# The early table of a routed feed-forward layer, made after eleven of sixteen groups instead of twelve

## The chip, the cores and the metric

The kernel runs on one core of a Trainium2 chip. The metric is the device time of one execution in microseconds (us). Before the change three runs gave 2174.46, 2169.46 and 2175.39 us, a median of 2174.46 us.

## What is computed

The input is eight sequences of 1024 tokens with 256 features, all in float32. The reference does two steps, each with a layer norm in front, a layer norm behind and the input added back:

```
x = x + _layernorm(attn(_layernorm(x), Wq, Wk, Wv, Wo))
x = x + _layernorm(ffn(_layernorm(x), router_weight, router_bias, gate_up_proj, ..., down_bias))
```

The attention is causal, with 16 heads of 16 features. The feed-forward layer has eight experts of 512 hidden features. A router gives each token a softmax over the experts. The two best experts are applied to the token, and their outputs are added with the router's weights.

## The kernel before, in words

**Attention (lines 542 to 1391).** A unit is one sequence b and four heads, so there are 32 units, u = 0 to 31. One pass of the loop at line 1299 computes the row maxima of unit u (scores `sa`, line 834; reductions on VectorE, lines 844 to 888) and, beside them, the weighted values of unit u-1 (scores `sb`, line 929; exponentials on ScalarE, line 941; masks on GpSimd, line 950; products `av`, line 970). A unit has nine steps k = 0 to 8, each in two pairs of heads. The last pass, u = 32, has only the values of unit 31.

The values of a unit need its negated maxima as extra rows of the queries. `rows` (line 796) reduces and transposes them on VectorE, and four copies (line 807) bring them into the query tile. The copies go through SyncE's queue (SP below), which takes its transfers in order.

**Work between the scores.** Whatever belongs to a finished half sequence (a group of 512 tokens, 16 groups t = 0 to 15) is written as generators that give up control with `piece(...)`: the output projection and first norm (`finish`, line 1017), the router (`route`, line 1074) and the tables (`table`, line 301). They stand in a list `back` as jobs. A planner, `pump` (line 1253), runs a step of a job when each engine has credit for the step's stated cost. The order of the list decides between jobs. The instructions of TensorE (PE), VectorE (DVE) and ScalarE (ACT) stand in the order in which this planner emits them. On GpSimd (POOL), the order of the source is kept by declared dependences.

`route` ranks the experts of each token (lines 1130 to 1149), counts with two matmuls (`cps`, line 1153), forms row numbers (lines 1160 to 1183) and scatters the normalized rows of the group into a DRAM array `xsd`, sorted by expert, with eight indirect DMAs on POOL (line 1194). It does so one group after the other.

**Tables.** The experts' work is cut into tiles of 256 rows of one expert. A table says for each tile which expert and which rows of `xsd` it has. There are two. The early one is made inside `route` of a chosen group, after so many groups as `NT - LATE` says (NT = 16 groups). It has the first EARLY = 16 tiles, which are whole already. The last table is made after all 16 groups and has the rest. In both, `table` runs some 10 to 30 small VectorE instructions between three matmuls: `segps` (line 363), `firstps` (line 371) and `tabps` (line 417). The early one has a fourth, `takenps` (line 438), and only behind it is the table marked as known (line 440).

As soon as the early table is known, in the last maxima pass (u = 31), `load_early` (line 1277) reads table entries on SP and loads the rows of the first four tiles. If it isn't known at the end of that pass, the planner is left aside (lines 1383 to 1386):

```
if u == B * NG - 1 and not early:
    while NT - LATE not in known:
        emit(back, back[0])
    load_early()
```

**Experts (lines 1638 to 1738).** The tiles run one after the other: transposes `xtps` (line 1448), four quarters of gate and up products `gu` (line 1470) with VectorE, ScalarE and POOL work behind them (lines 1479 to 1492), then the down products `dn` (line 1510), a bias add on VectorE (line 1518) and two scatters of results on POOL (line 1524). `dn` of tile i-1 stands between the quarters of tile i. `load_tile` (line 1417) is called two tiles ahead and issues on SP the rows, the weights `wg` and `wd` and the biases. While i + 2 < 16, `pump` is still called between the quarters, so that the rest of the routing is done beside the first tiles. When tile 16's loads come up, at the begin of tile 14, everything left must be done (line 1669):

```
if nth + AHEAD == EARLY:
    finish_all()
```

`finish_all` (line 1270) emits all that is left of the jobs without a look at credits. Ahead of the last table `fill_tails` (line 275) writes zeros behind the rows of each expert with eight DMAs of 258 KB on SP, and tiles loaded later wait for these.

Of the kernel before, what the change touches and what calls it, by code (L numbers as in the profile page):

```python
# [58 lines left out]
def attn_moe_kernel(  # L59
# [199 lines left out]
    def ahead_of(load, group):  # L259

        tc.add_to_no_dep_group(group, load.ins)

    def loaded(ap, most, engine=mybir.EngineType.SP):
        return nc.values_load(
            ap, engines=[engine], min_val=0, max_val=most,
            skip_runtime_bounds_check_because="tables made on the chip from counts of tokens",
        )

    def slot_rows(at, n=TN):
        return xs_dram[ds(at, n * P), :].rearrange("(n p) d -> p n d", p=P)  # L270
# [4 lines left out]
    def fill_tails():  # L275
# [9 lines left out]

    LATE = 4
    tables = {
        n: const.tile([1, 2, NTILES], I32, name=f"table{n}") for n in (NT - LATE, NT)  # L290
    }

    regions = {
        n: const.tile([P, NTILES], F32, name=f"regions{n}") for n in (NT - LATE, NT)
    }
# [246 lines left out]
    with ExitStack() as attn:  # L542
# [675 lines left out]
        def emit(kind, job):  # L1218
            job.run(now)
            if job.done:  # L1220
                kind.remove(job)
# [55 lines left out]
        def load_early():  # L1277

            flat = x_buffer("early")
            for i in range(IN_X):  # L1280
                early[i] = flat[:, ts(i, XS)].rearrange("p (n d) -> p n d", n=TN)
                at = loaded(tables[NT - LATE][:, 1, i : i + 1], E * R)
                ahead_of(nc.sync.dma_start(out=early[i], in_=slot_rows(at)), "xs")
# [3 lines left out]
        with tc.manual_schedule(  # L1287
# [11 lines left out]
            for u in range(B * NG + 1):  # L1299
# [12 lines left out]
                for k in range(K):  # L1312
                    if second:

                        for c in {t[0] for t in STEPS[k][2]}:
                            while not rows_of[u - 1, c].done:
                                emit(urgent, rows_of[u - 1, c])
                    if u == B * NG - 1 and not early and NT - LATE in known:
                        load_early()
# [63 lines left out]
# [3 lines that stand above are left out]
# [22 lines left out]
    def first_weights(i):  # L1408
        tab = tables[NT - LATE if i < EARLY else NT]
        e = loaded(tab[:, 0, i : i + 1], E - 1)  # L1410
        wg = m3.tile([P, KT, 2 * FF], F32, tag="wg", name=f"wg_{i}")
        nc.sync.dma_start(
            out=wg, in_=gate_up[ds(e, 1), :, :].rearrange("o (t p) f -> p (o t) f", p=P)
        )
        begun[i] = e, wg
# [360 lines left out]
```

## Time and profile before

| | |
|---|---|
| runs, us | 2174.46, 2169.46, 2175.39 |
| the profiled execution, us | 2167.24 |
| its span in the profile, us | 2165.1 |
| PE busy | 2057.3 us, 95% of the span |
| DVE busy | 1708.3 us, 79% |
| ACT busy | 1062.7 us, 49% |
| POOL busy | 1051.7 us, 49% |
| mean granted PE clock | 0.985 |
| end of the last `sb` scores beside maxima (unit 30) | about 1347.3 us |
| the early table written (line 421) | 1352.1 us |
| first expert tile's transposes (line 1448) | 1382.3 us |
| the last table written (line 421) | 1553.9 us |

The timeline lists instructions of one engine in order of time. A row has the start, the time from the first start to the last end, the engine, the line, the operation, the tiles it writes and reads, how many records are merged in it, and in brackets how long the engine had been idle before and what ended this. A float32 matmul shows as two records. The granted clock is 1.00 at full speed. A window row has, for a stretch of time, the busy time of each engine, the mean granted clock and the DMA share.

### The profile page before, as it was taken

How to read it: one execution, taken by the hardware profiler on the slowest of the kernel's cores; microseconds unless marked ns; L12 is line 12 of the kernel's file. 1: busy time of each engine (PE TensorE's matmuls, PEld its weight loads, DVE VectorE, ACT ScalarE, POOL GpSimd, SP SyncE). 2: the span in 40 equal slices, each digit the busy share in tenths (PEclk: the TensorE clock that was granted, in tenths of full speed). 3: DMA queues.
4: the chain of work that ended last, by engine and by line, in shares of the span. 5: the costliest groups of instructions: out<-in, count | busy, mean ns of one | idle time of the engine just before them, and what ended most of it. 6: DMA issues, size and time to landing. Idle time of an engine off the chain costs nothing.

```text
span 2165.1 us, 44591 instructions
## 1 busy us (share of the span) xinstructions
PE 2057.3 (95%) x16205; PEld 1262.3 (58%) x16205; DVE 1708.3 (79%) x4091; ACT 1062.7 (49%) x2072; POOL 1051.7 (49%) x1213
## 2 busy tenths in 40 slices
PE   7999999999999999999999998999999999999995
PEld 3444444444544434434534443678888888888884
DVE  4786886986887887887888788678778888877776
ACT  3566665666666655656655665433123232222222
POOL 3421653472474455354544645456544444444443
PEclk9999999999999999999999999999999999999998
DMA  4101102112112111112111111656867777876784
GB/s 123 23 16 44 35 26 63 32 46 46 42 32 69 24 41 46 48 36 58 46 39 41 44 39 36 207 189 208 259 242 266 269 246 262 291 241 231 268 286 150
DMA packets 147096, 254.85 MB, mean 118 GB/s; under 512 B 21504, under 2 KB 106008, under 8 KB 144952
## 3 DMA queue, kind: packets, MB, share of 16 engines
q1 hardware_dynamic: 133128, 217.01, 32.5%
q0 software_dynamic: 12528, 34.36, 4.3%
q8 instruction: 129, 2.11, 0.4%
q14 instruction: 95, 0.78, 0.1%
q10 hardware_dynamic: 1216, 0.58, 0.1%
HBM read 171.13 MB, written 55.63 MB: 105 GB/s over the span
## 4 chain that ended last, share of the span: by engine, by line
PE 71%; DVE 17%; POOL 5%; issue 3%; DMA 2%; ACT 2%; SPq 0%; DVEq 0%; ACTq 0%; POOLq 0%
PE sa L834 18%; PE gu L1470 15%; PE av L970 10%; PE dn L1510 8%; PE sb L929 6%; PE pjk L740 3%; PE yps L1031 3%; PE pjq L740 3%; PE vps L726 3%; DVE mx L850 2%; DVE sa L844 2%; DVE gate L1479 1%; PE xtps L1448 1%; DVE mx L888 1%; DVE acc L1586 1%
## 5 line engine op out<-in xcount | busy, mean ns | idle before, releaser
L941 ACT ACTIVATE pT<-sb 128x512 f32<-128x512 f32 x1134 | 616.2, 595 | 394.2 <-PE sb L929 360.6
L929 PE MATMUL sb<-qP,kP 32*128 32x512 f32 (+3 forms) x3072 | 703.6, 528 | 13.8 <-ACT pT L941 11.0
L834 PE MATMUL sa<-kP,qP 32*128 32x512 f32 (+3 forms) x3072 | 655.2, 526 | 25.5 <-DVE mx L844 12.6
L1470 PE MATMUL gu<-xsT,wg 128*128 128x256 f32 (+1 forms) x2208 | 487.5, 373 | 3.3 <-ACT xsT L1450 1.9
L1470 PEld LDWEIGHTS gu<-xsT,wg 128*128 128x128 f32 x2208 | 407.6, 191 | 59.3 <-ACT xsT L1450 4.3
L850 DVE TENSOR_REDUCE mx<-sa 128x2 f32<-128x1024 f32 x256 | 310.6, 1215 | 116.7 <-PE sb L929 96.6
L950 POOL TENSOR_SCALAR_AFFINE_SELECT pT<-pT 128x512 f32<-128x512 f32 x256 | 164.6, 659 | 468.2 <-ACT pT L941 456.1
L834 PEld LDWEIGHTS sa<-kP,qP 32*128 32x128 f32 x3072 | 226.8, 185 | 248.1 <-issue 100.0
L1481 ACT ACTIVATE sig<-gate 128x256 f32<-128x256 f32 (+1 forms) x276 | 112.8, 409 | 522.2 <-DVE gate L1479 492.0
L970 PE MATMUL av<-pT,vpad 128*32 128x256 f32 (+1 forms) x5120 | 350.0, 370 | 5.0 <-DVE avs L981 3.0
L1486 POOL TENSOR_TENSOR sig<-sig,gate 128x256 f32<-128x256 f32 (+1 forms) x276 | 195.4, 715 | 321.4 <-ACT sig L1481 317.4
L929 PEld LDWEIGHTS sb<-qP,kP 32*128 32x128 f32 x3072 | 294.9, 186 | 46.2 <-ACT pT L941 20.5
L970 PEld LDWEIGHTS av<-pT,vpad 128*32 128x32 f32 x5120 | 117.1, 109 | 292.7 <-issue 233.9
L1510 PE MATMUL dn<-wd,act 128*128 128x256 f32 x1064 | 257.7, 382 | 14.0 <-DVE act L1491 11.5
L1510 PEld LDWEIGHTS dn<-wd,act 128*128 128x128 f32 x1064 | 194.6, 190 | 45.6 <-DVE act L1491 19.4
L844 DVE CUSTOM_DVE_ANT_0 sa<-sa,cmask 128x512 f32<-128x512 f32 x256 | 177.7, 699 | 40.2 <-PE sb L929 20.8
L1479 DVE TENSOR_SCALAR gate<-gu,bs 128x256 f32<-128x256 f32 (+1 forms) x276 | 128.8, 467 | 86.2 <-PE gu L1470 70.7
L1491 DVE SCALAR_TENSOR_TENSOR act<-up,sig 128x256 f32<-128x256 f32 (+1 forms) x276 | 131.9, 478 | 49.3 <-POOL sig L1486 45.5
L1194 POOL DMA_INDIRECT xsd<-xn,slots x128 | 129.1, 1009 | 64.2 <-DVE xn L1190 34.8
L1524 POOL DMA_INDIRECT ytd<-ys,places x133 | 134.9, 1014 | 48.8 <-issue 26.9
L869 ACT COPY edge<-sa 128x512 f32<-128x512 f32 x192 | 113.0, 589 | 41.1 <-DVE mx L859 19.9
L888 DVE TENSOR_REDUCE mx<-edge 128x8 f32<-128x1024 f32 x96 | 115.7, 1205 | 17.9 <-POOL edge L883 17.9
(243 smaller groups left out, 2327.4 us busy)
## 6 DMA issues: line engine op xcount, KB each, us to landing
wg<-_L_ffn_gate_up_proj_dram SPq DMA_DIRECT2D x69, 1024.0 KB
wd<-in_L_ffn_down_proj_dram SPq DMA_DIRECT2D x69, 512.0 KB
xs<-xsd SPq DMA_DIRECT2D x60, 258.0 KB
yy<-ytd SPq DMA_DIRECT2D x15, 1024.0 KB
bs<-biasd SPq DMA_DIRECT2D x69, 132.0 KB
x<-in_L_attn_x_dram SPq DMA_DIRECT2D x16, 512.0 KB
aT<-avn SPq DMA_DIRECT2D x256, 32.0 KB
x1d<-y SPq DMA_DIRECT2D x16, 512.0 KB
```

The source lines that it names most:

```text
L834: nc.tensor.matmul(ps[:, hh, ds(at, w)], lhsT=qP[r, ts(i, P)], rhs=kP[r, ds(c * QC, w)], start=True, stop=True,)
L844: nc.vector.tensor_tensor_reduce(out=ps[:, hh, :], in0=ps[:, hh, :], in1=cmask, scale=1.0, scalar=NEG, op0=ALU.add, op1=ALU.max, accum_out ...
L850: nc.vector.tensor_reduce(mx[:, heads, i, 2:3], ps, AX.X, ALU.max)
L888: nc.vector.tensor_reduce(mx[:, :, of_two(k)[0], 1], d, AX.X, ALU.max)
L929: nc.tensor.matmul(banks[hh][:, ds(at, QC - off)], lhsT=kP[r, ts(j, P)], rhs=qP[r, ds(c * QC + off, QC - off)], start=True, stop=True,)
L941: nc.scalar.activation(pT[:, 2 * pair + hh, :], banks[hh], AF.Exp)
L950: in_order(nc.gpsimd.affine_select(out=d, in_=d, compare_op=ALU.is_ge, fill=0.0, base=0, pattern=[[0, HG], [1, P]], channel_multiplier=-1,))
L970: nc.tensor.matmul(av[ds(hh * HS, HS), ds(off + a - at, z - a)], lhsT=vp[:, j, ds((g * HG + hh) * VS, HS)], rhs=pT[:, hh, a:z],  start=c n ...
L1470: nc.tensor.matmul(ps[:, half, :w], lhsT=wg[:, kt, ds(half * FF + f * P, P)], rhs=xT[:, kt, :], start=(kt == 0), stop=(kt == KT - 1),)
L1479: nc.vector.tensor_scalar(gt, ps[:, 0, :w], bs[:, f : f + 1], LIMIT, ALU.add, ALU.min)
L1486: in_order(nc.gpsimd.tensor_tensor(sg, sg, gt, ALU.mult))
L1510: nc.tensor.matmul(pss[n][:, 0, :], lhsT=act[:, f, ts(n, P)], rhs=wd[:, f, :], start=(f == 0), stop=(f == FT - 1),)
```

## The change

```
@@ -285,7 +285,7 @@
-    LATE = 4
+    LATE = 5
     tables = {
         n: const.tile([1, 2, NTILES], I32, name=f"table{n}") for n in (NT - LATE, NT)
     }
```

`LATE` has no other use than to name the early table, so this table is made behind the routing of the eleventh group (t = 10) instead of the twelfth (t = 11). The number of tiles that it hands out stays 16. The counts of the twelfth group no longer enter it. The last table still counts all groups. The same instructions are issued, apart from one constant block that `memset` clears (40 columns instead of 32 at line 356), but the jobs stand in another order, and so the planner places what follows elsewhere.

More of the change, by code (lines that the diff above doesn't have):

```diff
@@ L283, in fill_tails @@
             apart(nc.sync.dma_start(out=slot_rows(at), in_=zeros), "xs")
-    LATE = 4
+    LATE = 5
     tables = {
```

## The prediction

> **What bounds the kernel now.** I read the page first, then the timeline of PE and DVE around the two tables, then windows of the same stretches.
>
> ```profile
> PE 2057.3 (95%) x16205; PEld 1262.3 (58%) x16205; DVE 1708.3 (79%) x4091; ACT 1062.7 (49%) x2072; POOL 1051.7 (49%) x1213
> PE   7999999999999999999999998999999999999995
> ```
>
> PE is busy nearly throughout, and both kernels issue the same matmuls. So time can only change where PE waits or where its clock is lowered. One slice falls to 8: number 25, where attention ends. The PE timeline there:
>
> ```profile
> 1347.84 0.38 PE L371 MATMUL firstps<-seg,before 128*128 128x2 f32 x2
> 1351.28 0.82 PE L417 MATMUL tabps<-two,ones 128*128 128x144 f32 x2 [3.06 <-DVE two L414]
> 1353.36 0.57 PE L438 MATMUL takenps<-each,ones 128*128 128x8 f32 x2 [1.26 <-DVE each L435]
> 1353.86 2.09 PE L929 MATMUL sb<-qP,kP 32*128 32x512 f32 x8
> 1355.88 1.94 PE L970 MATMUL av<-pT,vpad 128*32 128x256 f32 x16
> ...
> 1358.15 2.09 PE L929 MATMUL sb<-qP,kP 32*128 32x384 f32 x16
> ```
>
> The early table isn't ready when the maxima end. Its last steps are emitted back to back, and PE waits for VectorE twice. The matmuls behind it run at half speed: eight `sb` take 2.09 us, later 1.14. The windows agree (the clock is the number behind POOL's bracket):
>
> ```profile
> 1350.00:1355.00 5.00, 2.46 (x12) 1.52 (x12) 2.24 (x12) 0.00 (x0) 0.00 (x0) 0.50 0.10 17
> 1355.00:1360.00 5.00, 5.00 (x41) 2.00 (x33) 0.57 (x3) 2.00 (x3) 1.38 (x2) 0.50 0.65 196
> 1360.00:1365.00 5.00, 5.00 (x81) 2.38 (x77) 3.48 (x10) 4.61 (x9) 2.61 (x3) 0.98 0.03 7
> ```
>
> The second place is where the last table is made, during expert tiles 12 and 13:
>
> ```profile
> 1536.98 0.70 PE L1510 MATMUL dn<-wd,act 128*128 128x256 f32 x2 [1.93 <-DVE up L1483]
> 1537.51 3.48 PE L1470 MATMUL gu<-xsT,wg 128*128 128x256 f32 x8
> ...
> 1544.82 0.28 PE L363 MATMUL segps<-ident,new 128*128 128x1 f32 x2
> ...
> 1558.50 3.69 PE L1470 MATMUL gu<-xsT,wg 128*128 128x256 f32 x16 [1.36 <-DMA wg<-_L_ffn_gate_up_proj_dram]
> ```
>
> Here the table's steps lie between the quarters. `segps` doesn't wait. What is lost is one wait for VectorE, a slow quarter behind it (3.48 us against 1.89), and one late weight load.
>
> **What the change moves.** I compared the emitted order of both kernels. The early table is now spread over the end of unit 30 and unit 31: `segps` behind the `av` of step 7 of unit 30's maxima, `tabps` behind step 2 of unit 31, `takenps` in step 6. `load_early` comes at step 7, so the forced stretch is gone. The routing of group 11 stands behind the table's steps and slips by about half a unit. Group 12's transposes move from unit 31 to just before the first expert tile, and all later groups slip too: the counting matmuls of group 15 from tile 10 to tile 12. `fill_tails` moves from the end of tile 11 to the end of tile 13, and the last table from tiles 12 and 13 into `finish_all`, between the last `gu` of tile 13 and the first of tile 14, all three matmuls with nothing between them. A forced table is exchanged for another, longer one.
>
> **Gains, against the profiled execution's 2167.24 us** (span 2165.1 us and 2.1 around it; the median of the runs, 2174.46, is 7.2 higher, so I carry the difference over):
> - The two waits: 3.06 + 1.26 = 4.3.
> - The clock behind them: `tabps` 0.82 against 0.41 at 1552.84, `sb` 2.09 against 1.14, `av` 1.94 against 1.07, `sb` 2.09 against 1.15 (1365.33), together 3.2.
> - At tile 12, the 1.93 wait, which follows from eight table instructions on VectorE (1533.28 to 1535.71) ahead of the quarter's own, and its clock: 3.48 - 1.89 and 0.74 - 0.60 for `xtps`, together 3.7.
> - The late weights of tile 14, 1.4. SP issued them at 1551.01 because the zeros of `fill_tails` (issue 1534.14 to 1543) held the loads behind them until 1550.07. In the new order the next load behind the zeros is tile 16's. Even 16 us of blocking ends before its rows are due, a tile and a half (10.8 us each, from 1565.49 to 1576.29 and on) behind the table. I put that at nothing; the cover gone, it would cost what exceeds this slack.
>
> Sum of gains: 12.6.
>
> **Losses.**
> - The forced last table. Its VectorE queue from the end of `dn` 12, with start-to-start times of the same rows in the old place: bias add 0.6, tails and first table steps 2.4, gate, up and product 1.1, lines 328 to 333 0.7, lines 338 to 354 1.5, together 6.3. PE has 1.7 of work beside it (one quarter), so `segps` waits 4.6. `firstps` waits about 0.3 for the copy of line 368. `tabps` waits for lines 375 to 402 (1546.89 to 1548.79) and 405 to 414 (1549.91 to 1551.38), 3.4. Together 8.3. Behind `tabps` VectorE has 17 more instructions (3.5) ahead of tile 14's gate, and `dn` 13 needs a product behind that; two slow quarters cover it.
> - The clock behind these waits. The nearest row is the forced early table: waits of 4.3 lost 3.2. Lower bound 1.7 (what the wait of 1.93 lost), upper 6.2 (the whole slow stretch, 1353.86 to 1360, at half speed twice over). I take 3.2.
> - A new wait at the start of the last unit. Its scores now follow at once, and step 2 needs the last maxima rows. The reduction ends at 1348.35, the four copies are issued from 1349.52, the last at 1351.6. How long they take to land isn't shown. At the start of the kernel copies issued from 20.32 to 22.74 were used at 24.72, so at most 2.6 from the last issue. So the rows are there by 1354.2 at the latest, wanted at about 1352.6 (1347.9 plus four groups of 1.1 and a bit): bounds 0 and 1.6, and I take 1.3, near the only row. ACT waits with it, and POOL's masks too.
> - VectorE in units 30 and 31, which it nearly fills (19.2 of 20 us busy from 1300). Behind unit 31's maxima it had 16 table instructions that now lie inside, about 3.0, less statistics that leave, 1.4. On the other side POOL loses some 14 us there (three scatters, seven norms, two adds and a power), and the chain of waits ran through POOL from 1324 to 1335. I take 0, bounds -2 and +2.
> - One more group routed beside the tiles. Three groups cost waits of 3.8 from 1408 to 1495 (for ACT and VectorE), 1.25 each. Part of group 12 is done earlier; 1.0, bounds 0 and 3. Its exponential brings two table loads on ACT (1.28 each, as at 1416.73 and 1418.42), behind which PE showed no wait.
>
> Sum of losses: 8.3 + 3.2 + 1.3 + 0 + 1.0 = 13.8. Net **+1.2 us**: 2168.4 for an execution like the profiled one, 2175.7 beside the median.
>
> The early table itself hands out the same tiles: counted from the reference's inputs, each expert has at least 1174 tokens after eleven groups and 1276 after twelve, and the first 16 tiles are two for each expert in both.
>
> On the clock, the row at 1536.98 shows that a wait of 1.93 already lost 1.7. [...]
>
> **Rivals.**
> - *Units 30 and 31 get shorter* because POOL no longer delays the edge masks and the counting matmuls no longer wait (2.35 at 1303.10). For: the chain through POOL. Against: VectorE was idle for hardly 3 us there and gets more work. Worth 2.35 + 1.10 + 1.43, and 1.12 for a mask wait at 1368.16 in the last unit, 6.0: net -4.8, or -6.3 if the clock loss is 1.7: 2169 beside the median.
> - *Slower: VectorE falls behind in tiles 0 to 13.* Group 12's ranking and slots, about 9 us, used to fill an idle VectorE in the last unit (12 of 20 us busy from 1360). Now they come between quarters. It decides when VectorE is about 2 us late as a `dn` is due; each such place cost 1.93 + 1.7 at tile 12. For: 18.8 of 20 us busy from 1420, 18.2 from 1500. Against: 11.7 from 1400, and the planner's credits. Two places: +7.3, net +8.5: 2183.
> - *Nothing moves in time*: the forced stretch only changes its place and all unknowns cancel: 2174.5.
>
> **How the numbers follow.** Forecast 0.50, units shorter 0.20, VectorE late 0.22, nothing 0.08. About 0.3%, 6.5 us, is what a measurement can tell from no change. Beyond it fall, on the fast side, 0.02 of the forecast and 0.12 of the first rival (where one more bound is free); on the slow side 0.03 of the forecast and 0.20 of the second. So faster 0.14, within 0.63, slower 0.23. The forecast's own bounds are -4.6 (1.2 less 1.5 clock, 1.3 rows, 2 units, 1 routing) and +8.5 (1.2 plus 3.0, 0.3, 2 and 2): 2170 to 2183. The range reaches to the first rival with a free rows wait and free routing, -8.6, and to the second with 2 more in the units, +10.5: 2166 to 2185.
>
> **What would show it.** Right: no wait at `tabps` in unit 31; `sb` at 1.1 us from the start of the last unit; a wait of about 1 us in its step 2; first tile about 8 to 10 us earlier; then waits of about 4.6 and 3.4 at `segps` and `tabps` between tiles 13 and 14 and `gu` at half speed behind. Wrong: `segps` hardly waiting, a clock that stays at 1.00 there, rows of tile 16 late behind the zeros, or several `dn` waits in tiles 0 to 12.

## The result, and the profile after

Beside each other on the same chip, the changed kernel takes 2176.35 us (median of 22 runs, 2169.70 to 2182.75) and the kernel before 2168.97 (22 runs, 2161.10 to 2175.39). The ratio is 1.0034, with a 95% interval of 1.0023 to 1.0046: 7.4 us slower (5.0 to 10.0). The profiled execution took 2180.28 us with a span of 2178.2. Of the 13.1 us between the two spans, 4.9 lie ahead of the `lps` of group 11 (line 1107), which starts at 1274.63 before and at 1279.48 after. Up to there, and for some 20 us more, the order of both is the same. Behind it the change costs 8.2.

The page of the changed kernel, engine totals and PE's 40 slices (ACT's two instructions more are loads of an activation table, 10 instead of 8, 1.28 us each; e4 comes back to them):

```profile
PE 2068.3 (95%) x16205; PEld 1268.4 (58%) x16205; DVE 1710.6 (79%) x4091; ACT 1066.1 (49%) x2074; POOL 1051.1 (48%) x1213
...
PE   7899999999999999999999989899899999999995
```

Three inner slices now fall to 8: number 24, number 26 (1361 to 1416 us, the last unit and the first tiles) and number 29 (1525 to 1579, the last table). The dip of before, at the early table, is gone. The PE timeline around the early table and the start of the last unit:

```profile
1326.38 0.51 PE L417 MATMUL tabps<-two,ones 128*128 128x144 f32 x2
...
1341.27 0.36 PE L438 MATMUL takenps<-each,ones 128*128 128x8 f32 x2 [1.07 <-DVE each L435]
...
1351.91 1.23 PE L929 MATMUL sb<-qP,kP 32*128 32x512 f32 x6 [0.32 <-ACT pT L941]
...
1356.15 2.03 PE L929 MATMUL sb<-qP,kP 32*128 32x256 f32 x16
```

`tabps` doesn't wait and `takenps` still waits 1.07. The last unit starts at full speed. The late maxima rows show as one stretched group, 2.03 us where the neighbouring group of 16 (1354.08) takes 1.15. Windows of the same stretch (clock behind POOL's bracket):

```profile
1350.00:1355.00 5.00, 4.68 (x48) 1.86 (x48) 4.26 (x15) 3.09 (x5) 1.57 (x3) 1.00 0.09 30
1355.00:1360.00 5.00, 4.99 (x65) 2.36 (x60) 2.49 (x5) 4.00 (x6) 3.79 (x5) 1.00 0.08 28
```

The clock stays at 1.00, where it was 0.50 twice. From group 11's `lps` to the first expert tile it takes 97.0 us instead of 107.7. What is lost again lies in the tiles. PE in tile 1:

```profile
1391.25 1.99 PE L1470 MATMUL gu<-xsT,wg 128*128 128x256 f32 x8 [1.45 <-ACT xsT L1450]
1396.11 0.53 PE L1153 MATMUL cps<-chosen,before 128*128 128x32 f32 x2 [2.87 <-DVE chosen L1149]
1396.45 0.61 PE L1153 MATMUL cps<-chosen,ones 128*128 128x32 f32 x2
1396.87 3.32 PE L1470 MATMUL gu<-xsT,wg 128*128 128x256 f32 x8
```

And between the last `gu` of tile 13 and the first of tile 14:

```profile
1564.49 0.59 PE L363 MATMUL segps<-ident,new 128*128 128x1 f32 x2 [6.69 <-DVE new L354]
...
1570.26 0.82 PE L417 MATMUL tabps<-two,ones 128*128 128x144 f32 x2 [3.07 <-DVE two L414]
1570.87 5.01 PE L1470 MATMUL gu<-xsT,wg 128*128 128x256 f32 x16
```

```profile
1560.00:1565.00 5.00, 0.51 (x3) 0.52 (x3) 4.12 (x15) 0.42 (x1) 3.67 (x4) 0.50 0.98 340
1565.00:1570.00 5.00, 1.94 (x9) 1.77 (x8) 2.69 (x16) 0.00 (x0) 0.00 (x0) 0.50 1.09 323
1570.00:1575.00 5.00, 4.74 (x15) 4.08 (x16) 3.65 (x23) 0.13 (x1) 0.14 (x1) 0.63 0.76 182
```

From the first tile's `xtps` to the seventeenth's it takes 213.5 us (1376.52 to 1589.97) instead of 194.0 (1382.29 to 1576.29). After that both go at 10.8 us a tile. So 10.6 us are won in front and 19.5 lost in the tiles. Of both, some 2.9 us are matmuls that only moved from units 31 and 32 into tiles 0 and 1 (`lpsT`, `lps`, `cps`, a part of `yps`).

### The profile page after: what moved, and what is told of

Its sections match the earlier page's. It is cut to its first block, busy times and chain, and to the rows that moved or that the text cites. A ratio compares the mean times of both kernels' runs of the same rounds, so it can differ in the third digit from the quotient of the medians.

```text
span 2178.2 us, 44599 instructions
## 1 busy us (share of the span) xinstructions
PE 2068.3 (95%) x16205; PEld 1268.4 (58%) x16205; DVE 1710.6 (79%) x4091; ACT 1066.1 (49%) x2074; POOL 1051.1 (48%) x1213
## 4 chain that ended last, share of the span: by engine, by line
PE 70%; DVE 17%; POOL 5%; issue 3%; ACT 2%; DMA 2%; DVEq 0%; ACTq 0%; SPq 0%; POOLq 0%
PE sa L834 18%; PE gu L1470 15%; PE av L970 10%; PE dn L1510 8%; PE sb L929 6%; PE pjk L740 3%; PE yps L1031 3%; PE pjq L740 3%; PE vps L726 3%; DVE mx L850 3%; DVE sa L844 2%; DVE mx L888 1%; DVE gate L1479 1%; POOL xsd L1194 1%; PE xtps L1448 1%
## 5 line engine op out<-in xcount | busy, mean ns | idle before, releaser
L929 PE MATMUL sb<-qP,kP 32*128 32x512 f32 (+3 forms) x3072 | 705.9, 526 | 12.2 <-ACT pT L941 11.2
```

The costliest lines, as they stand in the source:

```text
L929: nc.tensor.matmul(banks[hh][:, ds(at, QC - off)], lhsT=kP[r, ts(j, P)], rhs=qP[r, ds(c * QC + off, QC - off)], start=True, stop=True,)
```

## Experiments

"Lead" is the time from group 11's `lps` to the first `xtps`, "tiles" that from the first to the seventeenth `xtps`. Both are of one profiled execution, and by up to 3 us they depend on which: e1 has before's order up to the first tile, and its lead is 2.9 shorter. "Time" is the ratio to before with its interval. Ratios compare runs on the same chip: e1 to e4 had one on which before takes 2135.78 us, e5 to e8 and e12 one with 2167, e9 to e11 one with 2163.40. A difference to before that is given in us with an interval is the ratio's, times before's median there; the medians themselves differ from it by up to 3.4 us (e7).

In the edits, `after` is the number of calls of the planner that must pass before a step may run, the four numbers of `pump` are the credit in us that a call gives to PE, VectorE, ScalarE and GpSimd, and `f` counts the quarters of a tile from 0.

| kernel | time against before | lead, us | tiles, us |
|---|---|---|---|
| before | | 107.7 | 194.0 |
| changed | 1.0034 (1.0023 to 1.0046) | 97.0 | 213.5 |
| e1 last table held back, in before | 1.0057 (1.0041 to 1.0073) | 104.8 | 207.4 |
| e2 changed, more credit | 1.0063 (1.0047 to 1.0078) | 95.7 | 215.6 |
| e3 changed, counting later | 1.0049 (1.0033 to 1.0064) | 97.4 | 215.2 |
| e4 changed, no exponential in tile 1 | 1.0045 (1.0027 to 1.0062) | 95.7 | 213.2 |
| e5 changed again | 1.0035 (1.0021 to 1.0049) | 97.1 | 211.9 |
| e6 changed, table in tile 14 | 1.0023 (1.0005 to 1.0040) | 97.0 | 213.3 |
| e7 thirteen groups | 1.0079 (1.0052 to 1.0106) | 119.9 | 199.3 |
| e8 ten groups | 1.0043 (1.0026 to 1.0061) | | 215.2 |
| e9 group 12 in the tiles, in before | 1.0046 (1.0024 to 1.0069) | 106.8 | 202.0 |
| e10 early table in the last unit | 1.0007 (0.9991 to 1.0024) | 99.7 | 202.4 |
| e11 both tables planned | 0.9992 (0.9973 to 1.0012) | 99.7 | 198.0 |
| e12 the same, smaller portions | 0.9986 (0.9973 to 0.9999) | 101.6 | 200.0 |

(In e8 `lps` itself moved, so its lead isn't comparable.)

**e1, one part of the change alone: the forced last table.**

```
                 if nth + 1 in tables:
+                    if nth + 1 == NT:
+                        yield piece(after=200)
                     yield from table(nth + 1)
```

> The kernel before (early table after twelve groups), with one thing of the change alone: the last table is held back until it is forced between the last gu of tile 13 and the first of tile 14. Theory 1 (the forced table is the main price of the change): PE waits of 7 to 10 us in all at segps, firstps and tabps and about 3 us of lowered clock behind them; gone are the dn wait of 1.93 at tile 12 with its clock of 1.7, and the weight wait of 1.36. Net +5 to +9 us against before. Theory 2 (the table only shows a backlog of VectorE that comes from one more group routed beside the tiles): without that backlog segps hardly waits, net 0 to +3 us.

Measured: 12.2 us above before (8.8 to 15.6), beyond what theory 1 said, with an interval that just touches it. PE timeline:

```profile
1518.82 0.63 PE L1450 MATMUL xtps<-ident,xs 128*128 128x128 f32 x4 [3.33 <-DMA xs<-xsd]
...
1528.33 0.59 PE L363 MATMUL segps<-ident,new 128*128 128x1 f32 x2 [5.43 <-DVE new L354]
...
1534.12 0.82 PE L417 MATMUL tabps<-two,ones 128*128 128x144 f32 x2 [3.08 <-DVE two L414]
```

The waits of the forced table are 5.43 + 0.25 + 3.08 = 8.8, close to the 8.3 predicted for VectorE's queue alone. What theory 1 missed is a new wait of 3.33 for tile 14's rows, where before waited 1.36 for the same tile's weights: here too the load of these rows is issued behind the zeros of `fill_tails` (zeros from 1499.84, rows at 1515.90). In the changed kernel the zeros come after it. So the forced table by itself makes the kernel slower. With group 15 scattered late, as in the changed kernel, `segps` waits 1.3 longer.

**e2, the changed kernel with the last table in its old place.** Both `pump(0.6, 0.0, 0.6, 0.35)` became

```
+ pump(0.6, 0.3 if i > 1 else 0.0, 0.6, 0.45)
```

> The changed kernel with more credit for VectorE and GpSimd in the quarters from tile 2 on, so that the last table's matmuls stand in tiles 12 and 13 again, where they stood before; group 12 is still routed in tiles 0 and 1. Theory 1: the waits at segps and tabps (10.0 us) and their clock (3.0) go, a wait like that of before with its clock (up to 3.6) may come back; tiles 0 to 2 stay as slow as after the change. Against before -5 to 0 us. Theory 2: VectorE is late anyway, and the credit moves the waits into dn and gu of tiles 2 to 13: +4 to +8 us against before, as the changed kernel.

Measured: 13.5 us above before (10.0 to 16.7), worse than both. The waits at the table went, and others came. The largest is at a `dn` between the fourth and the fifth `xtps`. All engines there:

```profile
1384.66 0.96 POOL L1524 DMA_INDIRECT ytd<-ys,places  x1 [0.30 <-issue]
1385.92 0.96 POOL L1524 DMA_INDIRECT ytd<-ys,places  x1 [0.30 <-issue]
1386.91 1.05 POOL L517 TENSOR_TENSOR rstd<-ve,nhalf_seg 128x4 f32<-128x4 f32 x1
1387.94 0.71 POOL L1486 TENSOR_TENSOR sig<-sig,gate 128x256 f32<-128x256 f32 x1
1387.99 0.69 DVE L1062 SCALAR_TENSOR_TENSOR shift<-mv,rstd 128x4 f32<-128x4 f32 x1 [4.94 <-POOL rstd L517]
1388.60 0.41 DVE L1491 SCALAR_TENSOR_TENSOR act<-up,sig 128x256 f32<-128x256 f32 x1
...
1389.07 1.22 PE L1510 MATMUL dn<-wd,act 128*128 128x256 f32 x2 [5.63 <-DVE act L1491]
```

The bracket of `dn` names VectorE, but VectorE itself had been idle for 4.94, for `rstd` on POOL, which ran scatters first. Behind the instruction that waited for `rstd` stood `act` in VectorE's queue, and for `act` `dn` waited. The edit had raised POOL's credit too (0.35 to 0.45), so it doesn't show what VectorE's credit alone would do. Theory 2 holds for the effect (the waits move into the tiles), not for the engine, and the cost is above its range.

**e3, the wait at `cps` taken away.** In `route`, for the step of `cps`:

```
- yield piece(pe=0.6, dve=0.2, after=1 + 4 * more)
+ yield piece(pe=0.6, dve=0.2, after=5 if t == 12 else 1 + 4 * more)
```

> The changed kernel with the counting matmuls of group 12 emitted four pumps later, behind the dn of tile 0 instead of ahead of them. Theory 1 (PE's order, with the counting matmul ahead of work that is ready): the wait of 2.87 us at cps and the slow gu behind it (3.32 instead of 1.89) go, 3 to 4.5 us less than the changed kernel, so about +3 to +4 us against before. Theory 2 (VectorE itself is late in tile 1): the wait goes to the next matmul that needs VectorE, and the time stays within 1.5 us of the changed kernel's, +6 to +8 us against before.

Measured: 10.5 us above before (7.0 to 13.7). PE in tile 1:

```profile
1361.61 0.70 PE L1510 MATMUL dn<-wd,act 128*128 128x256 f32 x2 [1.42 <-DVE act L1491]
1362.14 0.30 PE L1153 MATMUL cps<-chosen,before 128*128 128x32 f32 x2
```

In place theory 1 is nearer: 2.87 at `cps` became 1.42 at `dn`, and the tile takes 12.9 us, against 14.3 to 17.6 in three executions with the changed kernel's tile 1. By the time it fails: all later routing slipped, and the gain was given back: the longest tile of group 13 takes 21.6 instead of 19.7, that of group 14 17.2 instead of 15.4, and `segps` waits 8.07 instead of 6.69.

**e4, no table load between the sigmoids of tile 1.**

```
- ... AF.Exp
+ ... AF.Sigmoid if t == 12 else AF.Exp
```

> The changed kernel with a sigmoid in place of the exponential for group 12 alone (its ranks stay the same, its weights do not), so that ScalarE loads no other table between two sigmoids there. If the table loads begin the delay of tile 1: the gu wait of 1.45 us for xsT goes, and of the 2.87 at cps at least half, as the gate behind that gu comes sooner; 3 to 5 us less than the changed kernel, +3 to +5 us against before. If VectorE's own queue is the cause: the 1.45 goes, the wait at cps grows by as much, and nothing is won, +6 to +8 us against before.

Measured: 9.6 us above before (5.8 to 13.2), nothing won.

```profile
1350.57 1.99 PE L1471 MATMUL gu<-xsT,wg 128*128 128x256 f32 x8 [0.61 <-ACT xsT L1451]
1355.44 0.38 PE L1154 MATMUL cps<-chosen,before 128*128 128x32 f32 x2 [2.88 <-DVE chosen L1150]
```

The table loads (1.28 us each at 1386.90 and 1388.44 in the changed kernel) made 0.84 of the wait of 1.45 for `xsT`. The wait at `cps` stays at 2.88; it neither halves nor grows, so neither forecast holds in its detail. It comes from VectorE's own queue, which in the changed kernel ran without a gap from 1388.46 to 1397.

**e5, the changed kernel again, beside e6 to e8.**

> The changed kernel itself, as the measure for its neighbours on the same chip. Expected +6 to +9 us against before, as in the first comparison (ratio 1.0034); the first tile 8 to 11 us earlier against the work ahead of it, 19 us more from the first to the seventeenth tile's turn.

Measured: 2175.38 against 2167.28 us, 7.6 above before (4.6 to 10.6). The waits are the same ones to within 0.03 us.

**e6, time instead of credit for the last table.** Both `5`s behind `first_ones else` became 3 and 2, and

```
-            if nth + AHEAD == EARLY:
-                finish_all()
...
+                if nth + AHEAD == EARLY and f == 2:
+                    finish_all()
+                    full_table[0] = True
+                    loads[order[nth + AHEAD]] = load_tile(order[nth + AHEAD])
```

> The changed kernel with no more credit in any tile: the last table gets time instead. Tile 16's loads are issued in the middle of tile 14 and not at its start, the table's segps and tabps are due three pumps after their VectorE work instead of five, and its steps may use the quarters of tile 14. Theory 1 (the forced table is the largest price; VectorE has room in tile 14): of 10.0 us of waits and 3.0 of clock at most 3 to 5 stay; 7 to 10 us less than the changed kernel, 3 us below before to 1 above it. Theory 2 (VectorE is late whatever the order): the waits go to dn and gu in tiles 13 to 15, less than 3 us won. Theory 3: tile 16's rows or weights come late, and xtps or gu of tile 16 waits for DMA.

Measured: 2172.26 us, 5.0 above before (1.1 to 8.7). That is 3.1 below the changed kernel's median in e5, with intervals that overlap. PE timeline:

```profile
1562.82 0.79 PE L1510 MATMUL dn<-wd,act 128*128 128x256 f32 x2 [1.70 <-DVE act L1491]
1565.40 0.56 PE L363 MATMUL segps<-ident,new 128*128 128x1 f32 x2 [1.80 <-DVE new L354]
...
1575.87 0.48 PE L417 MATMUL tabps<-two,ones 128*128 128x144 f32 x2 [2.96 <-DVE two L414]
```

10.0 us of waits became 6.5, spread over three places. From the `xtps` of tile 14 to that of tile 16 it takes 34.5 us, in e5 36.4. VectorE is busy for 4.79 of 5 us from 1560. This is nearer to theory 2. Theory 3 falls: nothing of tile 16 waits for DMA.

**e7, thirteen groups** (`LATE = 3`).

> The early table after thirteen groups. From the first tile's turn to the seventeenth's: 194 in before, and if a group routed beside the tiles costs 2.9 us of moved matmuls and 5 to 6 of waits and clock, 184 to 187 here; if its price is 1 us of waits as predicted, 190. The forced early table now also has group 12's scores and counting ahead of it: waits there grow from 4.3 to 7 to 12 us, and the first tile comes 6 to 12 us later than in before. In all -2 to +4 us against before by the first price, +3 to +8 by the second.

Measured: 17 us above before (11 to 23), above both ranges. In front, the forced stretch now begins with the counting:

```profile
1357.29 0.61 PE L1153 MATMUL cps<-chosen,before 128*128 128x32 f32 x2 [5.12 <-DVE chosen L1149]
...
1363.96 0.99 PE L363 MATMUL segps<-ident,new 128*128 128x1 f32 x4 [5.64 <-DVE new L356]
```

With `firstps`, `tabps` and `takenps` the waits are 14.4. And the tiles are not shorter by a group's price. Here the forecast's premise was wrong: before counts group 12 ahead of the first tile already (`cps` at 1372.88), so both kernels have the same three groups, 13 to 15, beside the tiles. They take 199.3 instead of 194.0, with one wait of 3.81 at a `dn` behind the same chain through POOL as in e2, and one of 3.38 for a transfer of the attention's output. The same groups have waits of 9.5 there instead of 4.6, so waits of the routing aren't a fixed price per group.

**e8, ten groups** (`LATE = 6`).

> The early table after ten groups; nothing is forced in the attention any more, but one more group is routed beside the tiles and the forced last table has group 15's counting ahead of it. If a group costs 5 to 6 us of waits and clock beside the tiles: 6 to 10 us more than the changed kernel. If only the forced table has a price: 1 to 3 us more.

Measured: 9.3 us above before (5.6 to 13.2), some 2 above the changed kernel and not separable from it. The premise was wrong here too: the emitted order shows the same four groups beside the tiles, 12 to 15, with group 12 one to two tiles later. The forced table begins with group 15's `cps` (a wait of 2.05) and `segps` waits 7.88. The run is no test of the price of a group.

**e9, the other part alone: group 12's ranking in the tiles, both tables in their old place.** In before, ahead of the division of the exponentials:

```
- yield piece(dve=0.6, after=1)
+ yield piece(dve=0.6, after=8 if t == 12 else 1)
```

> The kernel before, with the ranking and counting of group 12 held back until the expert tiles, so that its counting matmuls stand in tile 1 as in the changed kernel; both tables stay where they were in before. Theory 1 (work of VectorE that leaves the last unit for the first tiles is a price of the change by itself): the waits between the first and the twelfth tile, 4.6 us in before without those at the first tile's start, grow by 4 to 8, with 1 to 4 of clock: +5 to +10 us against before. Theory 2 (the forced last table is all of the price, and the planner hides a group's ranking as predicted): 0 to +2 us.

Measured: 10 us above before (5 to 15). The PE waits by cause, first tile to 1480 us:

```profile
PE cps L1153 <- DVE chosen L1149: 4.7, 2, 3.1
PE dn L1510 <- DVE act L1491: 3.3, 1, 3.3
PE gu L1470 <- ACT xsT L1450: 1.5, 2, 0.8
```

(Of the 1.5 at `gu`, 0.7 are the first tile's start, as in before.) Theory 1 holds. Up to tile 12 the waits are 11.9 instead of 4.6 (without those at the first tile's start), and the tiles take 8.0 us more, with a last table that isn't forced. The waits come at group 13's counting as well as at group 12's.

**e10, the early table planned in the last unit.** In before, the forced loop moves from the end of unit 31's pass to step 5 of the last one:

```
+                    if u == B * NG and k == 5:
+                        while NT - LATE not in known:
+                            emit(back, back[0])
-                    if u == B * NG - 1 and not early and NT - LATE in known:
+                    if u >= B * NG - 1 and not early and NT - LATE in known:
                         load_early()
```

> The kernel before, its early table still after twelve groups but no longer forced behind unit 31: its steps may use the last unit up to step 5, and the loads of the early rows follow it. Theory 1: the forced waits of 4.3 us and their clock of 3.2 go and the first tile comes 5 to 8 us earlier; the routing of groups 13 to 15 slips by about a tile and the last table is forced between tiles 13 and 14, +8 to +12 in the tiles; net +1 to +6 us against before. Rival: the early rows, asked for later, come too late for the first tile, which waits for DMA by 3 us or more, and nothing is won in front.

Measured: 1.5 us above before (-1.9 to +5.2). Theory 1 holds: the lead is 8.0 shorter and the tiles 8.4 longer. The rows are in time: the first tile waits 0.84 for VectorE as in before. So the forced early table was worth about what was predicted (4.3 and 3.2), without a table of fewer groups; against the leads of e9 and e1, where it is forced too, it is 7.1 and 5.1. And the tiles took it back.

**e11, both tables planned.** e10 with the later loads of e6, there after the second quarter (`f == 1`), and the same due times of 3 and 2.

> As its neighbour with the early table planned in the last unit, and the last table planned as well: due three pumps behind its VectorE work instead of five, and tile 16's loads issued after the second quarter of tile 14. Theory 1 (both forced stretches are prices, and VectorE has room for the last table in tiles 12 to 14): 3 to 8 us less than before. Theory 2 (VectorE is full in tiles 12 to 14 and late in any order): the waits come back at dn, segps and tabps there, 0 to +4 us against before.

Measured: 1.7 us below before (-5.8 to +2.6), undecided.

**e12, e11 in smaller portions.** A `yield piece(dve=0.6)` ahead of line 323, `tabps` due after 4, loads at `f == 2`.

> As e11, with the last table's VectorE work in smaller portions and its due times spread: the first portion is split in two, tabps is due four pumps behind its work, tile 16's loads follow the third quarter of tile 14. Theory 1 (PE waits where portions stand bunched ahead of what it needs): the waits of 1.91 at dn of tile 12 and of 2.23 at tabps, with the lowered clock behind the first, 6 us in all, fall below 2; 2 to 4 us less than e11 and 3 to 9 less than before. Theory 2 (VectorE is full there): the waits move by a quarter and keep their sum, time within 2 us of e11.

Measured: 3.0 us below before (0.2 to 5.9). This is the only version whose interval lies below before, and barely. The waits around the last table, e11 and then e12:

```profile
1538.64 0.70 PE L1509 MATMUL dn<-wd,act 128*128 128x256 f32 x2 [1.91 <-DVE up L1482]
...
1553.44 0.48 PE L417 MATMUL tabps<-two,ones 128*128 128x144 f32 x2 [2.23 <-DVE two L414]
```

```profile
1543.59 0.70 PE L1510 MATMUL dn<-wd,act 128*128 128x256 f32 x2 [0.99 <-DVE act L1491]
...
1553.17 0.38 PE L364 MATMUL segps<-ident,new 128*128 128x1 f32 x2 [3.26 <-DVE new L355]
```

4.1 in e11, 4.3 in e12: the waits changed places and kept their sum, as theory 2 says.

## Why the prediction was right and wrong

The median, 2176.35, is 0.65 from the forecast and inside the range. That flatters it. The forecast was +1.2 us beside three runs with a median of 2174.46; over 22 runs before has 2168.97, and the change costs 7.4. This is beyond the 6.5 set as the bound (its interval, from 5.0, reaches below), on the side that had a chance of 0.23, and near the net of +8.5 of the second rival. The terms, in us, each read from one profiled execution before and one after:

| step | predicted | measured |
|---|---|---|
| waits of the forced early table | -4.3 | -3.2 (1.07 stays at `takenps`) |
| its clock | -3.2 | -3.2 |
| `dn` wait of tile 12 and its clock | -3.7 | -3.7 |
| late weights of tile 14 | -1.4 | -1.4 |
| waits of the forced last table | +8.3 | +10.0 (6.69, 0.25, 3.07) |
| its clock | +3.2 | +3 (1.4 at `gu`, the rest at the table's matmuls) |
| maxima rows in the last unit | +1.3 | +0.9 |
| units 30 and 31 | 0 | -3.1 (waits 9.6 to 6.5, without `takenps`) |
| one more group routed beside the tiles | +1.0 | +6.0 waits, +1.8 clock |
| sum | +1.2 | +7 (8.2 between the profiles; the rest is not assigned) |

**Right:** every gain that was listed, its place and its size in waits. The two gains of clock, 3.2 and 1.7, agree with the profiled execution from which they were taken; other executions show less (last section). The order of the steps held: no wait at `tabps` in unit 31, full clock at the start of the last unit, the first tile 8 to 10 us earlier (10.6), the half-speed quarter behind the last table. The zeros of `fill_tails` held nothing up: the next load behind them (zeros issued from 1558.81 to 1568.88) was tile 16's, at 1576.23, and no row of tile 16 waits for DMA.

**Wrong: the term "one more group routed beside the tiles", 1.0 (bounds 0 and 3).** It measured 6.0 of waits (10.6 instead of 4.6, without the tables and the first tile's start), and 1.8 of clock behind them in tile 1. The mean wait of groups 13 to 15 had been taken as the price of another group. Two things were missed. The last unit, where VectorE had 12 of 20 us to do, took group 12's ranking for nothing; in tile 1 the same instructions stand in one queue with the quarters' own work. And what follows moves too: group 13, routed in another place among the tiles, has waits of 3.3 at its own matmuls (`x2ps`, `lpsT`, `cps`) instead of 0.6. e9 shows the term by itself (+8.0 in the tiles), and e4 that ScalarE's table loads make 0.84 of it at most. The second rival named this mechanism, its size (+7.3) and its point of decision. Its place was only partly right: PE waits first at `xsT` and at the counting matmul, not at `dn`. "Part of group 12 is done earlier" was the argument against it, and it wasn't enough: the ranking, the part that VectorE carries, wasn't done.

**Mis-sized: units 30 and 31**, put at 0 with bounds of -2 and +2. Here the first rival was half right. The waits of 2.35, 1.10 and 1.43 that it named went, and new ones of 1.17, 1.07 and 0.54 came (1304.85, 1307.62 and 1324.16), the first two of PE for VectorE's maxima. Net of the smaller ones it is -3.1; between e1 and e2 to e4, on another chip, it is -2.7. Without this gain the change would have cost some 3 us more.

**Mis-sized: the forced last table**, 10.0 instead of 8.3. e1, with group 15 done in time, has 8.8. In the changed kernel group 15's scatters stand between POOL's products, and VectorE waits for these (0.90 at 1556.44) ahead of the table's steps.

The two parts alone cost more than the change loses in its tiles (8.0 in e9 and 13.4 in e1 against 19.5 - 2.9 = 16.6), so they don't simply add. Of the 4.8 between, 3.3 are e1's wait for tile 14's rows, which the changed kernel doesn't have; the other 1.5 are within what the clock changes from one execution to another. Nor do the runs give a law for the price of a group's routing: e7 has the same three groups beside the tiles as before, and its waits there are twice as long.

## What to carry to other kernels

When work is moved from a stage in which its engine idles to one in which that engine is nearly full, price it by the queue that it joins, with all that is pushed behind it, and not by the mean wait of work that is already there. An order forced at one place can be given time at another without a change of what it computes (e10 did it in the last unit and won 8 us of lead), but e10 lost as much in the tiles, so the gain has to be measured at the end of the kernel. Where an engine is nearly full, finer portions and other due times may only move a wait: in e12 the sum stayed (4.1 and 4.3), in e6 it fell from 10.0 to 6.5.

## What the runs showed of the hardware

**The clock's loss behind the same waits differs from one execution to the next.** The changed kernel, e5 and e6 have the same instructions in tile 1, with waits of 1.45, 1.44 and 1.45 at `gu` and 2.87 each time at `cps`. Behind them the changed kernel's next `gu` takes 3.32. e5 and then e6:

```profile
1391.76 0.38 PE L1153 MATMUL cps<-chosen,before 128*128 128x32 f32 x2 [2.87 <-DVE chosen L1149]
...
1392.20 1.97 PE L1470 MATMUL gu<-xsT,wg 128*128 128x256 f32 x8
1394.01 1.89 PE L1510 MATMUL dn<-wd,act 128*128 128x256 f32 x8
```

```profile
1392.76 0.61 PE L1153 MATMUL cps<-chosen,before 128*128 128x32 f32 x2 [2.87 <-DVE chosen L1149]
...
1393.61 3.76 PE L1470 MATMUL gu<-xsT,wg 128*128 128x256 f32 x8
1397.16 3.03 PE L1510 MATMUL dn<-wd,act 128*128 128x256 f32 x8
```

From `xtps` of tile 1 to that of tile 2 the three take 16.0, 14.3 and 17.6 us. So what the clock took behind the wait of 2.87 was 0.1 (e5), 1.8 (changed) and 3.5 us (e6), against 1.89 for the `gu` and the `dn` and 0.38 and 0.39 for the two `cps`: not one number. The same holds for the rows from which the prediction took its clock terms. In e10 the `dn` of tile 12 waits 1.92, as in before (1.93), but the `gu` behind it takes 1.89 and not 3.48:

```profile
1537.64 0.70 PE L1509 MATMUL dn<-wd,act 128*128 128x256 f32 x2 [1.92 <-DVE act L1490]
1538.18 1.89 PE L1469 MATMUL gu<-xsT,wg 128*128 128x256 f32 x8
```

In e1 and e9, behind the same waits of 3.06 and 1.26 at the early table, only the first group of `sb` is slow (2.09); the next takes 1.15, where in before it takes 2.09. In tile 1 the granted clock differs as the times do: from 1395 to 1400 us it is 0.66 in the changed kernel and 0.55 in e6, and in e5 it is 1.00 from 1385 to 1400. What decides which it is isn't shown. Slow matmuls followed waits of 2.87 (2 us of work behind one of 1.45) and, in before, of 1.93; in e5 and e10 the `gu` behind 2.87 and 1.92 takes 1.97 and 1.89.

**Two of VectorE's smallest instructions took as long as GpSimd's beside them.** All engines in tile 1 of the changed kernel:

```profile
1390.80 0.78 POOL L1486 TENSOR_TENSOR sig<-sig,gate 128x256 f32<-128x256 f32 x1 [1.17 <-ACT sig L1481]
1390.91 0.69 DVE L1454 TENSOR_SCALAR far<-early 128x2 f32<-128x2 f32 x1
...
1391.54 0.72 POOL L1050 TENSOR_TENSOR y<-y,x 128x256 f32<-128x256 f32 x1
1391.64 0.64 DVE L1457 SCALAR_TENSOR_TENSOR far<-early,regions,far 128x2 f32<-128x2 f32 x1
```

The first `far` ends at 1391.60, within 0.02 us of POOL's product, the second at 1392.28, within 0.02 of POOL's sum. In tile 14, at 1556.78, beside an indirect DMA on POOL (1556.57 to 1557.75), they take 0.16 and 0.22. In before only the first `far` of tile 1 is slow: 0.69 at 1392.46, with its end at 1393.15 within 0.02 of that of POOL's product (1392.36 to 1393.13); the second takes 0.22. That these instructions were held by POOL's is an inference from the rows and not shown: no run takes POOL's work away. Against 0.16 and 0.22 the two add 0.95 us to VectorE's queue in tile 1, at the place where `cps` waits, and in before the one adds 0.53.
